# Seven half-size products at the border of layers 0 and 2, PSUM rings by hand, an earlier copy and a reordered start in a four-layer fp32 kernel

## The chip, the cores and the metric

One core of a Trainium2 chip runs the whole program in one launch. The metric is device time in microseconds (us), the median of the runs shown; lower is better. Engines are named as in the profile: PE is TensorE (PEld its weight loads), DVE is VectorE, ACT is ScalarE, POOL is GpSimd and SP is SyncE. L721 is line 721 of the kernel before.

## What is computed

Four images of 512 channels by 1024 tokens pass through four residual layers, all in fp32, each on a group-normalized input:

```python
x = x + attention0(gn(x))   # 8 heads; a head-mixing 8x8 product ahead of the softmax; instance norm; projection and bias
x = x + gate(gn(x))         # channel means -> a 9-qubit circuit simulation -> sigmoid gate per channel
x = x + attention2(gn(x))   # 8 heads; q, k and v with bias; softmax; projection and bias
x = x + memory(gn(x))       # 2048 items; the 8 best per token, softmax over them, weighted sum of rows
```

A projection is a product of a 512x512 weight matrix with a 512x1024 image.

## The kernel before

Channels lie as `[128, 4, 1024]`: partition p and block k hold channel 128k + p. A block is P = 128 channels, NB = 512 is the widest matmul, and KC = 4 blocks.

**Layer 0** goes image by image in STEPS = 32 steps of 32 queries, with seven more steps behind them (LAG = 7). `step` (L1436) writes out by hand what each engine gets in each step: scores, head mixing, exponentials, transposes and products with v, in a software pipeline. Nearly every instruction is wrapped in `pin`, which holds it behind the one traced before it on its engine; so the order on each queue is the order of the code. The products with v of four steps collect in one PSUM bank, `pv_bank`, and `take_out` (L590) copies it to SBUF on ACT in step 34 for tile 6 and in step 38 for tile 7, behind `piece`, which in those steps projects q of the next image. Small results (group sums, key sums, the gate's circuit) share one bank, `pt_bank`, through `small_ps` (L60). Work of the gate for the image before is a generator, `gating` (L861), that is taken one `yield` per step or per projected block (`state["behind"]`).

**The border.** After the last image's steps the kernel projects k (L1148) and v (L1155) of image 0 for layer 2, and then the last image's output of layer 0 (`put_out`, L729), each by 64 half-matmuls of 512 columns (in `put_out` 128 of 256 columns). `instance_norm` (L640) and `norm_quarter` (L666) stand between k and v. `put_out` adds bias and x from DRAM in 128x512 pieces and stores the sum.

**Layer 2.** Here the PSUM tiles come from two pools, `ps_s` (three tiles of two banks) and `ps_m` (two of one bank), opened once layer 0's tiles are released (L1590 to L1595). Score tiles, projections and small results all take the next free tile of `ps_s`. k, v and the output of the images after the first are already made by seven products of half-size blocks (`seven`, L1033): the operands are split in quarters, `weight_sums` (L1007) and `input_sums` (L1000) form sums of quarters on DVE, each of the seven products is 16 half-matmuls, and DVE adds or subtracts each product into the quarters of the result. `seven_out` (L1094) also finishes each quarter as it is complete (`done`, L1122): add x, statistics, store. The order of the products is

```python
SEVEN = (
    (1, ((0, 0, "="), (1, 1, "="))),
    (4, ((0, 0, "+"), (1, 0, "="))),
    (3, ((0, 1, "="), (1, 1, "+"))),
    (5, ((0, 0, "-"), (0, 1, "+"))),
    (2, ((1, 0, "+"), (1, 1, "-"))),
    (7, ((0, 0, "+"),)),
    (6, ((1, 1, "+"),)),
)
```

After `seven_out` the loop goes on with `scores2` (L1165): four score tiles in a row, each read by one exponential on ACT, and then `apply2` (L1206), the products with v of the unit before.

**Start.** `first` (L294) loads image 0 and w_q block by block on SP's queue, while nine small constants are loaded on ACT's queue. For each block DVE takes statistics, two tiny matmuls with `gavg` average them over groups (POOL does the arithmetic between them, L150 to L152, and the power -0.5, L119), DVE normalizes, and the products of q follow block by block (`multiply`, L330).

Of the kernel before, what the change touches and what calls it, by code (L numbers as in the profile page):

```python
# [41 lines left out]
def fast_net(ctx: ExitStack, tc: tile.TileContext, a: dict, out: bass.AP, flag: bass.AP):  # L42
# [19 lines left out]


    def chan(src, name):
        t = const.tile([P, KC], F32, tag=name, name=name)
        nc.scalar.dma_start(out=t, in_=src)
        return t

    gamma = const.tile([P, NH], F32, tag="gamma", name="gamma")
    nc.scalar.dma_start(out=gamma, in_=a["in_gamma"].partition_broadcast(P))  # L70
    beta = const.tile([P, NH], F32, tag="beta", name="beta")
    nc.scalar.dma_start(out=beta, in_=a["in_beta"].partition_broadcast(P))
    bproj = chan(a["b_proj"], "bproj")
    bq2 = chan(a["bq"], "bq2")
    bk2 = chan(a["bk"], "bk2")
    bp2 = chan(a["bp"], "bp2")
    fcb = chan(a["fc_b"], "fcb")

    fcw = const.tile([NQ, C], F32, tag="fcw", name="fcw")
    nc.scalar.dma_start(out=fcw, in_=a["fc_w"])  # L80
    qpar = const.tile([P, NL * NQ], F32, tag="qpar", name="qpar")
    nc.scalar.dma_start(out=qpar, in_=a["q_params"].partition_broadcast(P))
# [3 lines left out]
    ident = const.tile([P, P], F32, tag="ident", name="ident")  # L86
    make_identity(nc, ident)
    ones = const.tile([P, P], F32, tag="ones", name="ones")
    nc.gpsimd.memset(ones, 1.0)
# [13 lines left out]
    )  # L103
    NS = 32
# [71 lines left out]
    def place(at, name):  # L176

        return pairs[at % 3] if at is not None else ps_s.tile([P, 2, NB], F32, tag="sc", name=name)
# [115 lines left out]
    def first():  # L294

        I = img[0]
        xn = I["xn"] = xn_all
        w = I["w_q"] = eight_k([P, KC, C], "w_q0_0", 0)
        for k in range(KC):
            nc.sync.dma_start(out=xn[:, k, :], in_=x_v[0, :, k, :])  # L300
            nc.sync.dma_start(out=w[:, k, :], in_=a["w_q"][:, k, :])
        I["w_k"] = load_w("w_k", "w_k0_0", 1)
        I["w_v"] = load_w("w_v", "w_v0_0", 2)
        q = I["q"] = big("q", "q0_0")
        ybar = I["ybar"] = small.tile([P, KC], F32, tag="ybar", name="ybar0")
        parts, found = {}, {}

        def stats(k):
            mv = small.tile([P, 2], F32, tag="mv0", name=f"mv0_{k}")
            st = small.tile([P, 2, 6], F32, tag="bnst", name=f"st_a0_{k}")  # L310
            for i in range(2):
                pin(nc.vector.bn_stats(st[:, i, :], xn[:, k, i * NB:(i + 1) * NB]))
            pin(nc.vector.bn_aggr(mv, st.rearrange("p i s -> p (i s)")))
            parts[k] = group_coeffs_parts(mv[:, 0:1], mv[:, 1:2], f"a0_{k}")

        def means(k):
            next(parts[k])
            next(parts[k])

        def deviations(k):  # L320
            next(parts[k])
            found[k] = next(parts[k])

        def normalize(k):
            gm, rstd, dm = found[k]
            pin(nc.vector.tensor_scalar(
                xn[:, k, :], xn[:, k, :], gm, rstd, ALU.subtract, ALU.mult))
            pin(nc.gpsimd.tensor_mul(ybar[:, k:k + 1], dm, rstd))

        def multiply(k, m):  # L330
            for n in range(T // NB):
                pin(nc.tensor.matmul(
                    pairs[m][:, n, :],
                    w[:, k, m * P:(m + 1) * P], xn[:, k, n * NB:(n + 1) * NB],
                    start=(k == 0), stop=(k == KC - 1),
                ))

        stats(0)
        means(0)
        stats(1)  # L340
        deviations(0)
        means(1)
        normalize(0)
        for k in range(KC):
            if k + 2 < KC:
                stats(k + 2)
            multiply(k, 0)
            if k + 1 < KC:
                deviations(k + 1)
            multiply(k, 1)  # L350
            if k + 1 < KC:
                normalize(k + 1)
            if k + 2 < KC:
                means(k + 2)
        for m in range(2):
            put_q(q, m)(flat2(pairs[m]))
        for m in (2, 3):
            project(w, tokens(xn), m, m, put_q(q, m))
# [648 lines left out]
    def weight_sums(b, key):  # L1007

        w = img[b][key]
        a11, a21, a12, a22 = quarters(w, H)  # L1010
        s1, s6, s7 = places7[key]
        add7(s1, a11, a22)
        sub7(s7, a12, a22)
        add7(a12, a11, a12)
        sub7(s6, a21, a11)
        add7(a21, a21, a22)
        nc.sync.dma_start(out=w_sums[key], in_=w)
# [15 lines left out]
    def seven(b, key, src, multiply, view, block, begin, done=None):  # L1033
# [3 lines left out]
        b11, t6, t7, b22 = quarters(src, NB)  # L1037
# [3 lines left out]
        for i, (at, uses) in enumerate(SEVEN):  # L1041
            ps = ps_s.tile([P, 2, NB], F32, tag="sc", name=f"{key}_{b}_{at}")
            multiply(ps, *factors[at])
            for *ij, op in uses:
                if op == "=":
                    begin(*ij, ps)
                else:
                    (add7 if op == "+" else sub7)(block(*ij), block(*ij), view(ps))
            if done and i in LAST7:
                done(*LAST7[i][1])  # L1050
            yield

    def by_channels(ps, w, x):
        for m in range(2):
            for k in range(2):
                pin(nc.tensor.matmul(  # L1056
                    ps[:, m, :], w[:, k, m * P:(m + 1) * P], x[:, k, :],
                    start=(k == 0), stop=(k == 1)))

# [105 lines left out]
    def scores2(b, u, before=None):  # L1165
# [14 lines left out]
        for i, t in enumerate(range(t0, t0 + 4)):  # L1180
            sc = ps_s.tile([P, 2, NB], F32, tag="sc", name=f"sc_{nm}_{t}")
# [24 lines left out]
    def apply2(b, u, exp2=None):  # L1206
# [3 lines left out]
        if t0 == 0:  # L1210
            invert2(b)
            I["pv", m, n] = ps_m.tile([P, NB], F32, tag="mm", name=f"pv_c{b}_{m}_{n}")
# [27 lines left out]
    def invert2(b):  # L1240
# [7 lines left out]
        ps = ps_s.tile([P, 2, NB], F32, tag="sc", name=f"rs_{nm}")[:, 0, 0:NS]  # L1248
# [77 lines left out]
    def attention(b, tt, between=None):  # L1326
# [3 lines left out]
        for i, (lo, hi) in enumerate(  # L1330
                ((0, T), (T, T + NB), (T + NB, NI)) if (b, tt) == tiles[-1] else ((0, T), (T, NI))):
            sc = ps_s.tile([P, T], F32, tag="sc", name=f"at_{nm}_{i}")
# [54 lines left out]
    def read_last(b, tt, picked, dg):  # L1387

        got, et, rs, xr = picked
        tp = ps_m.tile([P, KC, P], F32, tag="mm", name=f"stp_{b}_{tt}")  # L1390
# [9 lines left out]
    def read(b, tt, picked):  # L1400
# [9 lines left out]
        tp = ps_m.tile([P, KC, P], F32, tag="mm", name=f"stp_{nm}")  # L1410
# [25 lines left out]
    def step(b, s, mid, piece):  # L1436
# [35 lines left out]
        if tiled:  # L1472
            apply(b, s - LAG)
        if not tiled or s >= STEPS:
            piece(b, s)
# [5 lines left out]
        if tiled and part == 3:  # L1481
            take_out(b, j)
# [57 lines left out]
    for b in range(B):  # L1540
# [18 lines left out]
        for s in range(STEPS, STEPS + LAG):  # L1559
            step(b, s, lambda b, s: next(state["behind"], None),  # L1560
                 lambda b, s: qs[s - STEPS](s + 1) if s < STEPS + KC else None)
            if s == STEPS + KC and not last:
# [5 lines left out]
        for m in range(KC):  # L1568
# [10 lines left out]
        if last:  # L1579
# [5 lines left out]
            for i in range(TC // 2):  # L1585
                take_v2(0, i, i + 2)
            for m in range(KC):
                put_out(b, m, m)

    stage.close()  # L1590
    pairs.clear()
    by_scalar.append(True)
    stage = ctx.enter_context(ExitStack())
    ps_s = stage.enter_context(tc.tile_pool(name="ps_s2", bufs=3, space=PSUM))
    ps_m = stage.enter_context(tc.tile_pool(name="ps_m2", bufs=2, space=PSUM))  # L1595

    def small_ps(name):
        return ps_s.tile([P, 2 * NB], F32, tag="sc", name=name)
# [81 lines left out]
    def check_range():  # L1680
# [3 lines left out]
        tps = ps_m.tile([P, NB], F32, tag="mm", name="tot")  # L1684
# [748 lines left out]
```

## Time and profile before

| | |
|---|---|
| Median of 3 runs | 2556.93 us (2554.43 to 2558.5) |
| The profiled execution | 2558.39 us, span of its records 2556.6 us |
| Granted TensorE clock, mean | 0.998 |
| PE busy | 2503.3 us |
| Seven products in layer 2, third image: k (with one small product in it), v | 24.7 us, 24.3 us |
| One projection of 64 half-matmuls | 27.6 us |

A line of a timeline gives start, duration, engine, line, operation, result and operands, how many instructions are merged, and in brackets the idle time ahead with what ended it. A line of waits gives who waited for whom, the total, how often, and the longest. An fp32 matmul shows as two records, so "x64" is 32 matmuls. A line of the stretches gives for PE, PEld, DVE, ACT and POOL the busy time and the count, then the granted clock, the share of the DMA engines and GB/s. A cold TensorE clock shows as 0.50.

### The profile page before, as it was taken

The numbers are of one execution on the slowest core, as the hardware profiler recorded it, in microseconds if no ns is written. First come the engines' busy times: TensorE is split into PE (matmuls) and PEld (weight loads), VectorE is DVE, ScalarE is ACT, GpSimd is POOL, SyncE is SP. The second block draws the span as 40 slices with busy tenths as digits, with TensorE's granted clock in tenths as the row PEclk, the third lists the DMA queues.
The fourth block names the chain that finished last, engine by engine and source line by source line (L and its number), as shares of the span: only waits on it lengthen the run. The fifth ranks groups of instructions, "written<-read, shape, count | busy, mean of one in ns | idle before, by whom it ended". The sixth has DMA issues, their size and how long they took to land.

```text
span 2556.6 us, 47828 instructions
## 1 busy us (share of the span) xinstructions
PE 2503.3 (98%) x18534; PEld 1180.8 (46%) x18534; DVE 1685.8 (66%) x2785; ACT 985.8 (39%) x1177; POOL 1192.5 (47%) x1700
## 2 busy tenths in 40 slices
PE   8999999999999999999999999999999999999998
PEld 3344534554355534555633533453353344444445
DVE  4599448872688438881267567576657648788875
ACT  1467336651666336651153145125314612121211
POOL 3266415553465425553074147117405617566655
PEclk9999999999999999999999999999999999999999
DMA  2578438872698428982301130121014046767665
GB/s 83 145 207 237 125 120 226 244 211 74 172 243 235 131 82 211 244 248 101 124 16 55 70 112 18 54 83 59 21 54 148 18 130 190 219 186 217 187 184 170
DMA packets 187211, 361.39 MB, mean 141 GB/s; under 512 B 32729, under 2 KB 96217, under 8 KB 182882
## 3 DMA queue, kind: packets, MB, share of 16 engines
q1 hardware_dynamic: 105744, 178.71, 22.6%
q0 software_dynamic: 49152, 142.79, 20.6%
q10 hardware_dynamic: 32082, 36.76, 5.3%
q8 instruction: 149, 2.44, 0.4%
q14 instruction: 84, 0.69, 0.1%
HBM read 186.96 MB, written 36.96 MB: 88 GB/s over the span
## 4 chain that ended last, share of the span: by engine, by line
PE 74%; issue 10%; POOL 7%; DVE 3%; ACT 3%; DMA 2%; POOLq 0%; SPq 0%; ACTq 0%; DVEq 0%
PE pair L192 10%; PE sc_c L1183 9%; PE pv_c L1220 9%; PE pv L532 8%; POOL got L1360 7%; PE pair L467 6%; PE pair L493 5%; PE pt L425 5%; PE pt L721 4%; PE q L192 3%; PE Wk L1056 3%; PE Wv L1063 3%; ACT e L500 2%; PE Wp L1056 2%; PE at L1335 2%
## 5 line engine op out<-in xcount | busy, mean ns | idle before, releaser
L482 POOL DMA_DIRECT2D s<-ss x512 | 258.2, 511 | 399.5 <-PE pair L493 113.4
L506 DVE STREAM_TRANSPOSE eT<-e 128x1024 f32<-128x1024 f32 x256 | 316.5, 1236 | 193.6 <-ACT e L500 193.0
L1360 POOL DMA_INDIRECT got<-in_mem,ix x256 | 279.5, 1092 | 213.2 <-issue 122.1
L1177 ACT ACTIVATE eT<-sc_c 128x1024 f32<-128x1024 f32 x256 | 248.0, 1022 | 330.7 <-PE sc_c L1183 204.8
L521 DVE BATCH_NORM_STATS2 st<-e 128x6 f32<-128x256 f32 x1024 | 350.7, 404 | 0.0
L500 ACT ACTIVATE e<-pair 128x1024 f32<-128x1024 f32 x256 | 250.7, 1022 | 167.5 <-PE pair L493 137.2
L1201 POOL TENSOR_TENSOR e<-eT 128x1024 f32<-128x1024 f32 x96 | 232.3, 2421 | 168.6 <-DVE out L1125 69.5
L467 PE MATMUL pair<-k,q 64*32 64x512 f32 x4096 | 267.4, 598 | 12.7 <-ACT e L500 12.7
L473 ACT COPY ss<-pair 128x1024 f32<-128x1024 f32 x256 | 247.3, 1020 | 77.5 <-DMA s<-ss 37.9
L532 PE MATMUL pv<-eT,v 128*64 128x128 f32 x4096 | 250.7, 276 | 8.9 <-ACT pv L592 8.9
L532 PEld LDWEIGHTS pv<-eT,v 128*64 128x64 f32 x4096 | 221.1, 137 | 76.7 <-issue 54.5
L1183 PE MATMUL sc_c<-q,k 64*128 64x512 f32 x1024 | 240.9, 607 | 3.1 <-DVE xr L684 2.3
L1220 PE MATMUL pv_c<-eT,v 128*64 128x512 f32 x1024 | 233.0, 597 | 0.0
L1202 DVE TENSOR_TENSOR eT<-eT,e 128x1024 f32<-128x1024 f32 x96 | 136.3, 1420 | 146.3 <-POOL e L1201 146.1
L1197 POOL TENSOR_TENSOR eT<-eT 128x1024 f32<-128x1024 f32 x32 | 77.8, 2433 | 206.8 <-ACT eT L1177 202.8
L1407 DVE SCALAR_TENSOR_TENSOR acc<-got,et,acc 128x512 f32<-128x512 f32 x210 | 157.9, 752 | 7.5
L493 PE MATMUL pair<-s,wmix 32*32 32x512 f32 x4096 | 160.6, 600 | 2.3 <-issue 2.1
L1183 PEld LDWEIGHTS sc_c<-q,k 64*128 64x128 f32 x1024 | 93.6, 187 | 141.0 <-issue 71.9
L1340 ACT COPY att<-at 128x1024 f32<-128x1024 f32 (+1 forms) x65 | 64.9, 999 | 219.7 <-PE at L1335 212.9
L467 PEld LDWEIGHTS pair<-k,q 64*32 64x32 f32 x4096 | 57.0, 105 | 179.9 <-ACT e L500 86.2
L1220 PEld LDWEIGHTS pv_c<-eT,v 128*64 128x64 f32 x1024 | 68.0, 137 | 136.8 <-issue 136.8
L1335 PE MATMUL at<-memT,xn_d 128*128 128x512 f32 x256 | 120.7, 594 | 0.0
(335 smaller groups left out, 3431.3 us busy)
## 6 DMA issues: line engine op xcount, KB each, us to landing
s<-ss SPq DMA_DIRECT2D x512, 128.0 KB
s<-ss POOLq DMA_DIRECT2D x512, 128.0 KB
rb<-r POOLq DMA_DIRECT2D x64, 128.0 KB
o<-o SPq DMA_DIRECT2D x32, 256.0 KB
xr<-in_x ACTq DMA_DIRECT2D x32, 256.0 KB
x<-xr SPq DMA_DIRECT2D x32, 256.0 KB
xr_c<-x SPq DMA_DIRECT2D x32, 256.0 KB
rb_c<-r SPq DMA_DIRECT2D x64, 128.0 KB
```

Source lines behind the costliest of these rows:

```text
L192: pin(nc.tensor.matmul(ps[:, n, :], w[:, k, m * P:(m + 1) * P], rhs(k, n), start=(k == 0), stop=(k == KC - 1),))
L467: pin(nc.tensor.matmul(sc[m * NS:(m + 1) * NS, r, :], q[r * HD:(r + 1) * HD, m, s * NS:(s + 1) * NS], k_[r * HD:(r + 1) * HD, m, n * NB:(n ...
L482: pin(relays[side].dma_start(out=s2[2 * m + r::NH], in_=ss[m * NS:(m + 1) * NS, r, :]))
L493: pin(nc.tensor.matmul(mixed(s, r // 2)[t * NS:(t + 1) * NS, r % 2, :].rearrange("p (qq k) -> p qq k", qq=2), wmix[r * NS:(r + 1) * NS], s ...
L500: pin(nc.scalar.activation(e[:, half].rearrange("p r qq k -> p (r qq k)"), flat2(mixed(s, half)), AF.Exp))
L506: pin(nc.vector.transpose(eT[:, j % 2].rearrange("p b (qq i r) x -> p i r qq b x", qq=2, i=4)[:, i, 2 * half:2 * half + 2], e[:, half].rea ...
L521: pin(nc.vector.bn_stats(st[:, i, 2 * half + r, qq, :], e[:, half, r, qq, :]))
L532: pin(nc.tensor.matmul(pv[r * HD:(r + 1) * HD, gp, :], I["v"][:, t, g * HD:(g + 1) * HD], eT[:, j % 2, t, :, 4 * g:4 * g + 4], start=(t == ...
L1177: pin(nc.scalar.activation(e, scs[len(es)], AF.Exp))
L1183: pin(nc.tensor.matmul(sc[:, r, :], I["k"][r * HD:(r + 1) * HD, m, t * P:(t + 1) * P], I["q"][r * HD:(r + 1) * HD, m, n * NB:(n + 1) * NB] ...
L1220: pin(nc.tensor.matmul(pv[r * HD:(r + 1) * HD, :], I["v"][:, t, h * HD:(h + 1) * HD], e[:, r, :], start=(t == 0), stop=(t == TC - 1),))
L1360: pin(nc.gpsimd.indirect_dma_start(out=got[:, i, :], out_offset=None, in_=a["mem"], in_offset=bass.IndirectOffsetOnAxis(ap=ix[:, i:i + 1], ...
```

## The change

1. **Start.** The nine constants are only listed (`held`), and their loads are issued behind those of x and w_q. x's first block is loaded in two halves. `ones` is set first, `ident` later. The arithmetic between the two group matmuls moves from POOL to DVE; the power stays on POOL. Matmuls of `ones` by `ones`, whose result isn't used, run ahead of and between the first steps (`warm`).
2. **take_out** goes ahead of `piece` in the steps from 32 on.
3. **Border.** k and v of image 0 and the last image's output of layer 0 are made by `seven`. Behind step 35 come five weight sums and three input sums; the others go between products. For the output, the sums are made of quarters of the normalized attention (`output_sums`), and `seven_collected` finishes each quarter. The gate's generator is taken seven times in k instead of four.
4. **Rings.** The pools of layer 2 are gone. `next_pair` hands out layer 0's three pairs in turn, `next_bank` its two single banks, and nothing is released in between.

The core of the diff:

```diff
+    turns = [1, 0]
+    def next_pair():
+        turns[0] += 1
+        return pairs[(turns[0] - 1) % 3]
+    later = []
+    def held(shape, name, src):
+        t = const.tile(shape, F32, tag=name, name=name)
+        later.append(lambda: nc.scalar.dma_start(out=t, in_=src))
         return t
...
+        for n in range(2):
+            nc.sync.dma_start(out=xn[:, 0, n * NB:(n + 1) * NB], in_=x_v[0, :, 0, n * NB:(n + 1) * NB])
         for k in range(KC):
-            nc.sync.dma_start(out=xn[:, k, :], in_=x_v[0, :, k, :])
+            if k > 0:
+                nc.sync.dma_start(out=xn[:, k, :], in_=x_v[0, :, k, :])
             nc.sync.dma_start(out=w[:, k, :], in_=a["w_q"][:, k, :])
+        for load in later:
+            load()
...
         def means(k):
-            next(parts[k])
-            next(parts[k])
+            mv = parts[k][0]
+            ps = small_ps(f"gps_a0_{k}")
+            pin(nc.tensor.matmul(ps[:, 0:1], gavg, mv[:, 0:1], start=True, stop=True))
+            dm, sq, gm = (column(name, k) for name in ("dm", "gsq", "gm"))
+            pin(nc.vector.tensor_sub(dm, mv[:, 0:1], ps[:, 0:1]))
+            pin(nc.vector.scalar_tensor_tensor(sq, dm, dm, mv[:, 1:2], ALU.mult, ALU.add))
+            pin(nc.vector.tensor_copy(gm, ps[:, 0:1]))
...
+        def warm(times):
+            for _ in range(times):
+                pin(nc.tensor.matmul(pairs[2][:, 0, 0:P], ones, ones, start=True, stop=True))
...
-        stats(0)
+        warm(11)
+        for i in range(2):
+            stats(0, i)
         means(0)
-        stats(1)
+        stats(1, 0)
+        warm(2)
         deviations(0)
+        stats(1, 1)
+        warm(2)
+        normalize(0)
         means(1)
-        normalize(0)
+        warm(2)
...
         for i, (at, uses) in enumerate(SEVEN):
-            ps = ps_s.tile([P, 2, NB], F32, tag="sc", name=f"{key}_{b}_{at}")
+            ps = next_pair()
...
+    def seven_collected(b):
...
+        def done(i, j):
+            for m in range(2 * i, 2 * i + 2):
+                part = dst[:, m, j * NB:(j + 1) * NB]
+                add7(part, part, rows.pop((m, j)))
+                pin(nc.vector.bn_stats(I["stb"][:, m, j, :], part))
+                if (i, j) in ((0, 0), (1, 1)):
+                    pin(nc.vector.bn_aggr(
+                        mv[:, m, :], I["stb"][:, m].rearrange("p i s -> p (i s)")))
+            nc.sync.dma_start(
+                out=x1[b][:, 2 * i:2 * i + 2, j * NB:(j + 1) * NB], in_=block(i, j))
...
         for i, t in enumerate(range(t0, t0 + 4)):
-            sc = ps_s.tile([P, 2, NB], F32, tag="sc", name=f"sc_{nm}_{t}")
+            sc = next_pair()
...
+        if s >= STEPS and tiled and part == 3:
+            take_out(b, j)
         if not tiled or s >= STEPS:
             piece(b, s)
...
-        if tiled and part == 3:
+        if tiled and part == 3 and s < STEPS:
             take_out(b, j)
...
+            if last and s == STEPS + 3:
+                border_places()
+                first7, rest7 = input_sums(nxt["xn"])
+                weight_sums(0, "Wk", False)
+                for fn in first7:
+                    fn()
...
+            for i, _ in enumerate(seven_k(0)):
+                if i == 0:
+                    for fn in rest7:
+                        fn()
+                if i == 2:
+                    weight_sums(0, "Wv", False)
+                if i == 4:
+                    weight_sums(b, "w_p", False)
+                next(state["behind"], None)
...
-            for i in range(TC // 2):
-                take_v2(0, i, i + 2)
-            for m in range(KC):
-                put_out(b, m, m)
-
-    stage.close()
-    pairs.clear()
+            sums7 = output_sums(b)
+            for i, _ in enumerate(seven_v(0)):
+                if i >= 2:
+                    for fn in next(sums7):
+                        fn()
+            seven_collected(b)
...
-    ps_s = stage.enter_context(tc.tile_pool(name="ps_s2", bufs=3, space=PSUM))
-    ps_m = stage.enter_context(tc.tile_pool(name="ps_m2", bufs=2, space=PSUM))
+    def next_bank():
+        turns[1] += 1
+        return (pv_bank, pt_bank)[turns[1] % 2]
```

## The prediction

> **What bounds it now.** I read the page's busy times, TensorE's waits, and then the timeline of the three places that the change touches. TensorE is busy throughout, so only its own work and its own waits count.
> ```profile
> PE 2503.3 (98%) x18534; PEld 1180.8 (46%) x18534; DVE 1685.8 (66%) x2785; ACT 985.8 (39%) x1177; POOL 1192.5 (47%) x1700
> ...
> PE 74%; issue 10%; POOL 7%; DVE 3%; ACT 3%; DMA 2%; POOLq 0%; SPq 0%; ACTq 0%; DVEq 0%
> ```
> The waits (us in total, times, longest) of TensorE; under them SP's longest:
> ```profile
> PE pv L532 <- ACT pv L592: 8.9, 15, 1.6
> PE sc_c L1183 <- DVE xr L684: 2.3, 1, 2.3
> PE Wk L1056 <- ACT k L1073: 2.0, 1, 2.0
> ...
> SPq L301 <- DMA bproj<-in_b_proj: 6.1, 1, 6.1
> ```
> Timeline of the start and of the border (start, us, engine, line, operation): TensorE, then VectorE.
> ```profile
> 11.31 3.78 PE L332 MATMUL pair<-xn_all,w_q 128*128 128x512 f32 x4 [0.97 <-DVE xn_all L326]
> 15.10 1.96 PE L332 MATMUL pair<-xn_all,w_q 128*128 128x512 f32 x4
> ...
> 1174.21 0.39 PE L886 MATMUL pt<-amp,turn 128*128 128x4 f32 x2
> 1174.53 3.71 PE L532 MATMUL pv<-eT,v 128*64 128x128 f32 x64
> 1178.86 0.38 PE L891 MATMUL pt<-amp,turn 128*128 128x2 f32 x2 [0.62 <-POOL amp L883]
> 1179.33 13.98 PE L192 MATMUL pair<-xn_all,Wk_n 128*128 128x512 f32 x32
> ...
> 1237.38 27.79 PE L745 MATMUL pair<-eT 128*128 128x256 f32 x128
> 1267.48 8.83 PE L1183 MATMUL sc_c<-q,k 64*128 64x512 f32 x32 [2.32 <-DVE xr L684]
> ...
> 1172.28 1.28 DVE L1145 TENSOR_SCALAR q<-pair,bq 128x1024 f32<-128x1024 f32 x1 [7.73 <-PE pair L192]
> 1173.48 0.35 DVE L559 RECIPROCAL ri<-pt 128x32 f32<-128x32 f32 x1
> 1174.63 0.16 DVE L130 COPY amp<-pt 128x4 f32<-128x4 f32 x1 [0.35 <-PE pt L886]
> ```
> The same four matmuls take 3.78 cold and 1.96 warm. At the border VectorE answers TensorE within a microsecond. k, v and the last output are 27.6 to 27.9 us of matmul each, then 2.32 of waiting. In stretches of 2 us, just after that wait (the figure after POOL's is the granted clock):
> ```profile
> 1267.00:1269.00 2.00, 1.52 (x4) 0.75 (x6) 1.48 (x5) 0.00 (x0) 0.00 (x0) 0.68 0.59 226
> 1269.00:1271.00 2.00, 2.00 (x8) 0.99 (x6) 0.00 (x0) 1.02 (x1) 0.00 (x0) 0.50 0.64 151
> ```
> End of a layer-2 output by seven products:
> ```profile
> 1491.85 3.60 PE L1056 MATMUL Wp<-eT 128*128 128x512 f32 x8
> 1495.38 4.69 PE L1183 MATMUL sc_c<-q,k 64*128 64x512 f32 x16
> 1500.00 3.65 PE L1220 MATMUL pv_c<-eT,v 128*64 128x512 f32 x16
> ...
> 1495.37 1.20 DVE L993 TENSOR_TENSOR out<-out,Wp 128x1024 f32<-128x1024 f32 x1
> 1499.84 1.17 DVE L993 TENSOR_TENSOR out<-out,Wp 128x1024 f32<-128x1024 f32 x1
> ```
> All four score tiles are done by 1500.0, though the last product's bank is read only from 1499.84 to 1501.01: the pool gave the third tile another bank.
>
> [...]
>
> **The change, part by part** (against the profiled 2558.39 us, span 2556.6; it lies 1.5 above the median, 2556.93).
>
> (1) Start. SP's second weight load waits 6.1 us for a small constant; the constants now go last, and x's first block comes in halves. VectorE begins on x at 5.60; I take 0.6 earlier for each of its two statistics and so an end of the first block's statistics near 5.8 instead of 7.13 (bounds 5.3 and 7.1). From there it is: group mean matmul 0.55, three small VectorE operations 0.6, second matmul 0.4 beside the next block's half (0.65), epsilon 0.15, power on POOL 0.6, second half and its aggregate 0.85 beside that, normalize 0.8: first product at about 9.6, not 11.31, gain 1.7. The power stays on POOL; what POOL loses (three operations of 0.19 and their handovers) is replaced by VectorE's. The warm-up matmuls (11, then 2 three times) fill TensorE's idle time: gain 3.78 - 1.96 = 1.8, or 0 if the clock falls back in between. Afterwards VectorE needs 3.65 per block and TensorE about 3.9, so the lead lasts. whp lands by 39, circuit's VectorE work ends at 56.4, k's first copy at 57.6, and its bank is wanted at 59.1: still hidden. **-3.6** (-1 to -5).
>
> (2) take_out ahead of the projection at step 34: the copy on ScalarE no longer stands behind q's copy. Waits removed for images 0 to 2: 1.59 + 1.47 + 1.47. Image 3's q goes through VectorE. **-4.5**.
>
> (3) Border. Each of three projections falls from 64 to 56 half-matmuls: 27.6 x 7/8 = 24.2, so -10.3 in all. Added ahead of them, on VectorE, after L1145: five weight sums 128x512 (0.69, in a row 3.35) and three input sums 128x1024 (1.22, in a row 3.5): 6.85 us. Behind them in the queue stand L559, L561 and L130. L886 writes the bank that L559 reads: it can't start before 1173.56 + 6.85 + 0.35 = 1180.8, where it started at 1174.21, and two of the pv groups (3.71) and L891 stand behind it. L130 comes at 1181.4; POOL then needs its issue (0.6), L605 (1.8) and the amplitude's operations (2.1), as it did between 1174.12 and 1178.8: L891 near 1186, or 1186.6 with the pv groups at half clock after 6.5 us idle. k begins at 1187.0 instead of 1179.3: +7.7. Bounds: 0, if other work ran there, and 9.
>
> k: 24.2, L901 0.5, L916 1.0 between products. VectorE: eight block sums from PSUM (1.22), two input sums, ten weight sums: about 19 us, beside it; but the last sum, L645 and POOL stand before L651: 2.2 after k's end. v begins at 1187.0 + 25.7 + 2.2 = 1214.9. In v, VectorE has 12 x 1.22 and twenty sums of 128x256 with runs of 16 (no row; between half and all of 128x512's 0.684; taken 0.38): 22.2, ends 3.2 late, harmless. The output begins at 1239.1, ends at 1263.3. Its VectorE work (8 x 1.22, eight times 0.69 + 0.69, aggregates) falls behind TensorE. From the output's begin: the fourth product ends at +13.8, its two sums at +16.15, the finished block (add and statistics of two halves, 2.7) at +18.85; fifth: sums +21.2, block +23.9; the sixth product (+20.7) has its sum at +25.1 and its block, aggregates and all 3.1, at +28.2; so the last product (+24.2) has its sum at +29.4. With a ring the third score tile takes the last product's pair: it waits from +26.05 to +29.45. pv then begins at +34.9, +36.3 with a chance of 0.8 for 3.4 us at half clock (1.7). That is 1275.4 where it was 1276.25: **-0.9** for all of (3), the pool's wait and its clock loss included; against before, k begins 7.7 later, v 5.1, the output 1.7. x's loads go through SP as the stores do; slots come free 3 us before use.
>
> (4) Rings in layer 2. The same third tile: three times it waits until 1501.05 and not 1497.7. Two tiles of 0.95 later pv starts at 1502.95, not 1500.0: +2.9, and 3.35 us idle is longer than the 2.32 that cost the clock: +1.7 x 0.8. 3 x 4.3 = **+12.8** (0 to 14). Elsewhere the ring asks for a tile whose reader is done (the exps end 0.5 us before pv does): 0.
>
> (5) Three more steps of the gate are taken in k, so its group sum leaves the first product gap of image 1, and product 4 finds a free pair: **-2.0** (0 to -2). The weights aren't stored three times: SP only, 0.
>
> Sum: -3.6 - 4.5 - 0.9 + 12.8 - 2.0 = +1.8: 2560.2 by the profiled run, **2558.7** from the median.
>
> **Rivals.** (B) No ring waits, because VectorE gets to the last sum in time: -12.8, and -4.7 in (3): 2541.2. The 4.5 us between L993's two lines speak against it. (C) The sums at the border run before L1145, where VectorE idles 7.73 us: 2558.7 - 7.7 = 2551.0. Against it: each is pinned behind the one before it. (D) Slower: a clock lost in the middle of a wait costs two windows, not one[...]; four waits by 1.7 make +6.8: 2565.5. [...] against, the 3.4 us it lasted at 1267.8. (E) B and C together, or the output sums hidden wholly: 2533.5.
>
> **How the numbers follow.** Chances: mine 0.56 (own range 2553 to 2564), B 0.12, C 0.14, D 0.12, E 0.06. The range reaches from B to D, 2541 to 2566. About 0.2% (5.1 us) is what a measurement can tell from no change. Faster: B, E, half of C, 0.02 of mine: 0.27. Slower: 0.10 of D, 0.12 of mine: 0.22. Same: 0.51.
>
> **What would show it.** First L332 line near 9.6 with 1.96; no wait over 0.3 at L592 in three images; a gap of 6 us before L886 and the eight sums ahead of L559; 24.2 per seven products; a wait of 3.4 us on L993's last sum in the third score tile at all four places, with clock 0.5 after it. If L886 isn't late, or the third tile isn't, the forecast is wrong by 8 or 13 us.

## The result, and the profile after

After: median 2568.61 us of 6 runs (2564.96 to 2570.74). Before: 2556.26 in six runs, the three above among them (2554.43 to 2559.41). The ratio is 1.0047, 95% interval 1.0035 to 1.0059: slower by 12.4 us. The forecast was 2558.7, and the result lies 2.6 above its range.

The profiled execution of after: span 2567.2. Its busy times and the shares of its chain:

```profile
PE 2508.8 (98%) x18568; PEld 1190.1 (46%) x18568; DVE 1725.9 (67%) x2857; ACT 992.2 (39%) x1189; POOL 1188.9 (46%) x1688
...
PE 72%; issue 8%; POOL 7%; DMA 5%; DVE 5%; ACT 2%; SPq 0%; POOLq 0%; ACTq 0%; DVEq 0%
```

TensorE has more busy time (2508.8 against 2503.3) though 24 of the border's 192 half-matmuls are gone: the warm-up matmuls and work at half clock stand in for them. The longest new and old waits of TensorE, then SP's:

```profile
PE pair L1301 <- DVE out L1028: 9.9, 3, 3.3
PE pt L921 <- DVE ri L594: 6.4, 1, 6.4
PE pv L567 <- ACT pv L627: 4.3, 12, 1.0
PE pair L1301 <- DVE sum L1028: 3.2, 1, 3.2
PE pt L936 <- POOL pr L931: 2.7, 1, 2.7
```
```profile
SPq L306 <- DMA gamma<-in_in_gamma: 2.2, 1, 2.2
...
SPq L307 <- DMA bproj<-in_b_proj: 1.4, 1, 1.4
```

The wait for `take_out`'s copy (L567) fell from 8.9 to 4.3. New are the waits of the score tiles (L1301) for VectorE, 13.1 in all, that of the gate's first rotation (L921), and one of the gate's sums (L936). SP still waits for constants.

A ledger, read from the start of the same TensorE instruction in both timelines, shows where the time came from:

| up to | before | after | difference | this stretch |
|---|---|---|---|---|
| q's last blocks of image 0 | 28.26 | 27.80 | -0.5 | start -0.5 |
| the key sum behind the last q of layer 2 | 1172.08 | 1167.22 | -4.9 | take_out -4.4 |
| first product with v of layer 2 | 1276.25 | 1275.93 | -0.3 | border +4.5 |
| first of the seven products for k, image 1 | 1413.58 | 1413.60 | 0.0 | +0.3 |
| first score unit of image 1 | 1467.51 | 1465.92 | -1.6 | gate's step -1.6 |
| third score unit of image 1 | 1503.58 | 1507.56 | +4.0 | ring +5.6 |
| the same, image 2 | 1722.69 | 1732.53 | +9.8 | ring +5.9 |
| the same, image 3 | 1941.82 | 1956.01 | +14.2 | ring +4.4 |
| last transpose of layer 3 | 2528.82 | 2543.01 | +14.2 | 0 |
| end of the span | 2556.6 | 2567.2 | +10.6 | the last tile -3.6 |

The last row isn't put down to the change: from that transpose to the end the profiled execution of before took 27.8 us, those of the changed kernel and of all the experiments 23.3 to 25.0, one with before's own layer 3 (e4) among them. Whether most executions of before end like the profiled one isn't known; +14.2 and +10.6 both lie within the interval of the medians' +12.4 (8.9 to 15.1).

A ledger compares one execution with one other. The nine kernels profiled here that have this start reach the first mark at 27.15 to 28.45 (before, and e4 with before's start: 28.26 and 28.48), and the twelve with the early copy take 1139 to 1143 for the second stretch (after 1139.4, before 1143.8). So these two rows are known only within some 1 and 4 us.

**Start.** TensorE, then VectorE:

```profile
9.53 0.38 PE L332 MATMUL pt<-mv,gavg 128*128 128x1 f32 x2 [1.51 <-DVE mv L324]
...
10.77 3.09 PE L360 MATMUL pair<-xn_all,w_q 128*128 128x512 f32 x4
```
```profile
7.88 0.69 DVE L322 BATCH_NORM_STATS2 st_a<-xn_all 128x6 f32<-128x512 f32 x1 [0.85 <-DMA xn_all<-in_x]
8.49 0.14 DVE L344 TENSOR_SCALAR gve_a<-pt 128x1 f32<-128x1 f32 x1
```

The first product begins at 10.77, not 9.6, and is cold for most of its length (3.09, with the clock at 0.50 up to 13.20; warm is 1.96). The epsilon of the first block (L344) stands behind statistics of the second block, which wait for its arrival at 7.88.

**Border.** TensorE, VectorE and GpSimd:

```profile
1175.77 0.56 PE L921 MATMUL pt<-amp,turn 128*128 128x4 f32 x2 [6.35 <-DVE ri L594]
1176.26 5.79 PE L567 MATMUL pv<-eT,v 128*64 128x128 f32 x64
...
1182.45 3.68 PE L1092 MATMUL pair<-eT 128*128 128x512 f32 x8
...
1192.31 0.35 PE L936 MATMUL pt<-pr,signs 128*9 128x1 f32 x8 [2.75 <-POOL pr L931]
...
1192.79 5.40 PE L1092 MATMUL pair<-eT,Wk_n 128*128 128x512 f32 x8
```
```profile
1167.42 1.28 DVE L1263 TENSOR_SCALAR q<-pair,bq 128x1024 f32<-128x1024 f32 x1 [7.73 <-PE pair L195]
...
1175.28 0.35 DVE L594 RECIPROCAL ri<-pt 128x32 f32<-128x32 f32 x1
```
```profile
1188.39 3.59 POOL L640 TENSOR_TENSOR o<-pv,rb 64x256 f32<-64x256 f32 x4
1192.06 0.20 POOL L931 TENSOR_TENSOR pr<-amp 128x4 f32<-128x4 f32 x1
```

The eight sums lie between q's copy and the reciprocal, as forecast; the idle 7.73 us ahead of that copy stayed empty. Not forecast: the gate's squares (L931) come behind four multiplications of the attention's output (L640); in before the order was the other way round. L931 isn't pinned, and no line of the diff moves it. TensorE waits 2.75 for it, and the product behind takes 5.40, not 3.70.

**Layer 2.** The first of its output borders on TensorE and VectorE, and stretches of 2 us (the figure after POOL's is the granted clock):

```profile
1493.78 2.38 PE L1301 MATMUL pair<-q,k 64*128 64x512 f32 x8
1499.46 3.78 PE L1301 MATMUL pair<-q,k 64*128 64x512 f32 x8 [3.30 <-DVE out L1028]
1503.17 4.45 PE L1338 MATMUL pt<-eT,v 128*64 128x512 f32 x16
```
```profile
1498.24 1.17 DVE L1028 TENSOR_TENSOR out<-out,pair 128x1024 f32<-128x1024 f32 x1
```
```profile
1496.00:1498.00 2.00, 0.16 (x2) 0.00 (x0) 1.93 (x4) 1.06 (x2) 0.64 (x1) 1.00 0.99 365
1498.00:1500.00 2.00, 0.54 (x2) 0.50 (x4) 1.63 (x4) 0.00 (x0) 1.71 (x1) 0.50 0.88 294
1500.00:1502.00 2.00, 2.00 (x6) 0.68 (x4) 1.97 (x3) 0.00 (x0) 0.00 (x0) 0.50 0.38 119
1502.00:1504.00 2.00, 2.00 (x6) 0.29 (x4) 1.90 (x5) 0.00 (x0) 0.00 (x0) 0.50 0.00 0
1504.00:1506.00 2.00, 2.00 (x10) 0.66 (x8) 0.18 (x1) 0.85 (x1) 0.00 (x0) 0.79 0.68 262
```

The third score tile waits for VectorE's last sum, as forecast. But the clock is at 0.50 from 1498 to beyond 1504. In the traces of before and after such a stretch lasts 3.41 us, called a window here, or twice that, 6.83 (unless the trace ends in it): this one, from 1498.00 to 1504.83, is two windows and not one.

### The profile page after: what moved, and what is told of

The parts are those of the page before. It is cut to its first block, busy times and chain, and to the rows that moved or that the text cites. A ratio compares the mean times of both kernels' runs of the same rounds, so it can differ in the third digit from the quotient of the medians.

```text
span 2567.2 us, 47940 instructions
## 1 busy us (share of the span) xinstructions
PE 2508.8 (98%) x18568; PEld 1190.1 (46%) x18568; DVE 1725.9 (67%) x2857; ACT 992.2 (39%) x1189; POOL 1188.9 (46%) x1688
## 3 DMA queue, kind: packets, MB, share of 16 engines
q8 instruction: 149, 2.44, 0.4%
## 4 chain that ended last, share of the span: by engine, by line
PE 72%; issue 8%; POOL 7%; DMA 5%; DVE 5%; ACT 2%; SPq 0%; POOLq 0%; ACTq 0%; DVEq 0%
PE pair L195 14%; PE pair L1301 9%; PE pv L567 8%; POOL got L1478 6%; PE pair L502 6%; PE pair L1092 5%; PE pair L528 5%; PE pt L460 5%; PE pt L1338 4%; PE pv L1338 4%; PE pair L1181 4%; PE pt L756 4%; DMA got<-in_mem,ix 3%; ACT e L535 2%; PE pair L1453 2%
## 5 line engine op out<-in xcount | busy, mean ns | idle before, releaser
L1295 ACT ACTIVATE eT<-pair 128x1024 f32<-128x1024 f32 x256 | 248.7, 1022 | 324.6 <-PE pair L1301 192.4
L1301 PE MATMUL pair<-q,k 64*128 64x512 f32 x1024 | 245.6, 618 | 13.4 <-DVE out L1028 9.9
L567 PE MATMUL pv<-eT,v 128*64 128x128 f32 x4096 | 252.7, 277 | 4.3 <-ACT pv L627 4.3
L567 PEld LDWEIGHTS pv<-eT,v 128*64 128x64 f32 x4096 | 223.2, 138 | 71.9 <-issue 55.2
L1320 DVE TENSOR_TENSOR eT<-eT,e 128x1024 f32<-128x1024 f32 x96 | 130.1, 1355 | 167.2 <-POOL e L1319 167.1
L1301 PEld LDWEIGHTS pair<-q,k 64*128 64x128 f32 x1024 | 94.8, 190 | 153.0 <-issue 71.7
L1458 ACT COPY att<-pair 128x1024 f32<-128x1024 f32 (+1 forms) x65 | 64.9, 999 | 220.9 <-PE pair L1453 220.8
L1453 PE MATMUL pair<-memT,xn_d 128*128 128x512 f32 x256 | 120.7, 594 | 0.0
L1453 PE MATMUL pair<-memT,eT 128*128 128x512 f32 x256 | 120.4, 593 | 0.0
L1453 PE MATMUL pair<-eT 128*128 128x512 f32 x256 | 120.3, 592 | 0.0
```

Source lines behind the costliest of these rows:

```text
L567: pin(nc.tensor.matmul(pv[r * HD:(r + 1) * HD, gp, :], I["v"][:, t, g * HD:(g + 1) * HD], eT[:, j % 2, t, :, 4 * g:4 * g + 4], start=(t == ...
L1295: pin(nc.scalar.activation(e, scs[len(es)], AF.Exp))
L1301: pin(nc.tensor.matmul(sc[:, r, :], I["k"][r * HD:(r + 1) * HD, m, t * P:(t + 1) * P], I["q"][r * HD:(r + 1) * HD, m, n * NB:(n + 1) * NB] ...
L1453: pin(nc.tensor.matmul(sc[:, i0 - lo:i0 - lo + NB], xn3[b][:, k, tt * P:(tt + 1) * P], memT[k][:, i0:i0 + NB], start=(k == 0), stop=(k == ...
```

## The experiments

All times are medians, against 2568.6 for after and 2556 to 2557 for the runs of before beside them; the interval is that of the ratio to before. Numbers of lines differ by up to twelve from one kernel to the next.

**e1, another pair for the score tiles.**

```diff
+    def spare_last():
+        t = turns[0]
+        spare[:] = [pairs[t % 3], pairs[(t + 1) % 3]] * 2
+        turns[0] += 2
     def next_pair():
+        if spare:
+            return spare.pop(0)
...
         run_out(seven(b, "Wp", I["o"], by_channels, lambda ps: ps, block, begin, done))
+        spare_last()
```
(and the same behind `seven_collected`'s products)

> The changed kernel, but the four score tiles behind the last of seven products take the two other pairs in turn, never the pair of that last product. Theory (the ring makes the third tile wait for VectorE's last sum, and the wait costs clock behind it): the waits of 3.18 and three times 3.30 us are gone, the clock stays at 1.00 there; counted from the traces 5.6 + 5.9 + 4.4 us come back at the three borders in layer 2 and about 4.9 (3.2 and half a window of 3.4) at the border of layers 0 and 2: 20.8 less than 2568.6, so 2548. Rival (VectorE's backlog is what counts and the wait only moves to the next user of that pair or to the exponentials): the products with v begin no earlier, at most the clock comes back, 2562 to 2568.

Measured 2550.78, ratio 0.9977 (0.9968 to 0.9987): 17.8 less. The first output border of layer 2:

```profile
1491.50 4.69 PE L1311 MATMUL pair<-q,k 64*128 64x512 f32 x16
1496.12 3.65 PE L1348 MATMUL pt<-eT,v 128*64 128x512 f32 x16
```

The wait is gone, and the matmuls take what they took in before (4.69 and 3.65); from the first score tile to the first product with v are 4.62 us, as in before (4.62), where after took 9.39. At the border of layers 0 and 2 the gain is 3.4 and not 4.9: 0.93 of waiting for the same sum remains, now at the fifth use. The ring, by itself, cost more than the whole loss of 12.4.

**e5, the wait kept and filled.**

```diff
             sc = next_pair()
+            if i == 2:
+                for _ in range(fill[0]):
+                    pin(nc.tensor.matmul(
+                        (pv_bank, pt_bank)[(turns[1] + 1) % 2][:, 0:P], ones, ones, start=True, stop=True))
+                fill[0] = 0
```
(`fill[0] = 10` behind `seven_out`'s products)

> The changed kernel, with ten unused matmuls of ones by ones (128x128, about 2.4 us) written into the idle bank between the second and third score tile at the three borders in layer 2; the wait for VectorE's last sum stays. Theory (beside the wait of 3.30 us the clock is lost for one or two windows, because TensorE idles): the third tile begins no earlier, TensorE's waits there fall to about 0.9, the clock stays at 1.00, and of the 5.6 + 5.9 + 4.4 us only three times 3.3 are left: 6 less, 2562.6. Rival (the low clock comes from something else than idling, or the wait alone made the loss): the clock falls all the same, 2568 to 2570.

Measured 2562.54, ratio 1.0025 (1.0017 to 1.0033): 6.1 less.

```profile
1494.21 2.38 PE L1309 MATMUL pair<-q,k 64*128 64x512 f32 x8
1496.52 2.50 PE L1305 MATMUL pt<-ones 128*128 128x128 f32 x20
1499.89 1.99 PE L1309 MATMUL pair<-q,k 64*128 64x512 f32 x8 [0.87 <-DVE out L1028]
1501.81 3.65 PE L1346 MATMUL pt<-eT,v 128*64 128x512 f32 x16
```

The third tile begins 5.68 after the first, just as in after (1499.46 - 1493.78), and then takes 1.99 and not 3.78. From the first score tile to the next score unit a border takes 11.2 in e5, 8.2 in before, and 13.8, 14.1 and 12.6 in after. So of the ring's 15.8 us in layer 2 8.9 are the delay that the waits make while the clock stays whole, and 6.9 are lost clock (6.1 between the medians), and the clock is lost because TensorE idles: with 2.50 us of the gap filled it stayed at 1.00.

**e9 and c5, the last sum ahead of the block work.**

```diff
-            if done and i in LAST7:
+            if done and i in LAST7 and i != 5:
+                if i == 6:
+                    done(*LAST7[5][1])
                 done(*LAST7[i][1])
```
(e9: after with this alone; c5: with the edits of e1 and e2 too)

> The changed kernel with its ring as it is, but VectorE adds the last product before it finishes the block of the product ahead of it (x, statistics), at all four borders. Theory (the wait needs both: a ring that gives the third score tile the last product's pair, and 2.9 us of block work ahead of that product's sum in VectorE's queue): the last sum ends about 2.9 us earlier, the third tile waits 0.4 instead of 3.3, the clock stays, and the same 15.9 at the three borders in layer 2 and about 3.4 at the border of layers 0 and 2 come back as with the other pairs: 2549. Rival (block work that comes later holds up the next image's statistics or the row buffers instead, and the waits appear further on): 2555 to 2568.

> The changed kernel with all three repairs: other pairs for the score tiles, the border's first sums one step earlier, the last product's sum ahead of the block work. Theory (the first and the third repair take away the same waits, so together they give hardly more than one; left are 0.9 + 0.2 us at the border of layers 0 and 2): 2537.8 - 1.1 = 2536.7, not to be told from c2_both's 2537.8. Rival (the repairs add up): 2520.

Measured 2560.97, ratio 1.0013 (1.0006 to 1.0020), 7.6 less than after, for e9 and 2547.70, 0.9963 (0.9949 to 0.9978), for c5; both expectations fell. The wait of the third tile is gone, but two units later there is a new one, at all four borders. c5's TensorE and VectorE:

```profile
1502.50 0.31 PE L1381 MATMUL pair<-s_c,same 128*64 128x32 f32 x4 [1.99 <-DVE s_c L1367]
```
```profile
1485.27 2.60 DVE L1254 SCALAR_TENSOR_TENSOR out<-xr_c,s,out 128x512 f32<-128x512 f32 x1
...
1489.37 3.37 DVE L1332 TENSOR_TENSOR eT<-eT,e 128x1024 f32<-128x1024 f32 x1
...
1493.51 2.23 DVE L1254 SCALAR_TENSOR_TENSOR out<-xr_c,s,out 128x512 f32<-128x512 f32 x1
```

The block work now begins while GpSimd adds exponentials (from 1484.96, 1489.20 and 1492.83, for 2.35 to 2.46 each). There it took 2.60 and 2.23, against 0.70 to 0.75 outside, and VectorE's own sum of exponentials (L1332) 3.37, against 1.22. Why they are stretched isn't shown. The key sums end 21.0 us after the first score tile behind the border, in c2 (below), where the first block's work comes earlier and only two operations are stretched (1.96 and 3.27), 17.4; TensorE wants them at 19.1. The waits of 2.0 to 2.4, four times, 8.4 in all, make most of the 10 us between c2 and c5. The rival was right: the wait moved.

**e2, the first sums one step earlier.**

```diff
-            if last and s == STEPS + 3:
+            if last and s == STEPS + 2:
```

> The changed kernel, but the border's eight first sums are written one step earlier, ahead of the last block's copy of q on VectorE. Theory (the eight sums hold back the reciprocal, and with it the matmul that writes the bank it reads): they fill VectorE's idle 7.7 us, TensorE's wait of 6.4 us falls under 0.5 and the half clock after it goes too; k begins 8 us earlier. The gate's squared amplitudes on GpSimd come only 6.6 us earlier, so the wait of 2.7 us ahead of the third product grows by about 1.3: 7 less, 2561.5. Rival (the sums then wait for something else, as the place they write is still read by the products with v): q's last copy comes late, k begins no earlier, 2567 to 2570.

Measured 2557.30, ratio 0.9999 (0.9990 to 1.0008): 11.3 less, 4 more than expected. VectorE, TensorE and GpSimd at the border:

```profile
1164.33 4.14 DVE L1028 TENSOR_TENSOR eT<-xn_all 128x1024 f32<-128x1024 f32 x3
1168.39 1.27 DVE L1263 TENSOR_SCALAR q<-pair,bq 128x1024 f32<-128x1024 f32 x1
1169.59 0.34 DVE L594 RECIPROCAL ri<-pt 128x32 f32<-128x32 f32 x1
```
```profile
1170.28 0.39 PE L921 MATMUL pt<-amp,turn 128*128 128x4 f32 x2
...
1175.42 3.68 PE L1092 MATMUL pair<-eT 128*128 128x512 f32 x8
```
```profile
1181.63 0.20 POOL L931 TENSOR_TENSOR pr<-amp 128x4 f32<-128x4 f32 x1
1181.78 3.60 POOL L640 TENSOR_TENSOR o<-pv,rb 64x256 f32<-64x256 f32 x4
```

The sums end just as q's block does, nothing waits for the reciprocal, and k begins 7.3 behind the key sum's matmul (1168.14), not 15.2. The expectation that L936's wait would grow was wrong: the squares stand ahead of the four multiplications again, and the wait is gone. From the key sum to the first product with v are now 96.3 us: after took 108.7, before 104.2.

**e6, the gate one product later.**

```diff
-                next(state["behind"], None)
+                if i > 0:
+                    next(state["behind"], None)
```

> The changed kernel, but the gate's generator is taken behind the second and later products of k only, six times instead of seven. Theory (what the border cost beyond the forecast is the wait of 2.75 us for the gate's squares on GpSimd ahead of the third product, and half a window of clock behind it, 1.7): the small product comes behind the third product of k, finds the squares done, and 4.4 come back: 2564.2. Rival (the matmuls behind it are slow for another reason, or the wait comes again at the next step of the gate): 2567 or more.

Measured 2568.23, ratio 1.0047 (1.0031 to 1.0063): no gain that the medians show. In the trace L936's wait is gone and v begins 43.6 behind the key sum, not 47.9: the 4.4 are there. Most of them were given back: the wait of 1.8 ahead of v, which cost no clock in after, cost a window at half clock here (5.39 for the first product behind it, where e2 has 3.70: 1.7), and with one gate step fewer at the border the wait of 1.96 in image 1 is back, where after had 0.69 (1.4 up to the first score unit). The 1.2 that are left are less than the medians can tell.

```profile
1211.00 0.39 PE L686 MATMUL pt<-ssqh,ones 128*128 128x8 f32 x2 [1.83 <-POOL ssqh L683]
1211.24 5.39 PE L1181 MATMUL pair<-eT 128*128 128x256 f32 x16
...
1417.44 7.13 PE L1092 MATMUL pair<-sums,Wk 128*128 128x512 f32 x16 [1.96 <-ACT k L1191]
```

**e7, the old border**: no first sums, no seven products for k, v and the last output.

```diff
-            if last and s == STEPS + 3:
+            if False:
...
-        for m in () if last else range(KC):
+        for m in range(KC):
...
-            seven_collected(b)
+            for i in range(TC // 2):
+                take_v2(0, i, i + 2)
+            for m in range(KC):
+                put_out(b, m, m)
```

> The changed kernel with the border of before: k, v and the last output by 64 half-matmuls each, no sums, the gate taken four times in k; start, copy and rings as changed. Theory (the new border, as it was built, costs 4.5 us more than the old one, counted between the last block of q and the first product with v): these 4.5 come back, the ring gives the first score tile another pair than the one that the old output's last addition reads, which saves its wait of 2.3 us and half a window of clock, 4 in all, and the gate's small product in image 1 costs 1.6 again: 2568.6 - 4.5 - 4 + 1.6 = 2561.7. Rival (the seven products save what was forecast, 0.9, and the loss is elsewhere): 2567 or more.

Measured 2564.64, ratio 1.0028 (1.0017 to 1.0038): 4.0 less than after, between the two. From the key sum to the first product with v it takes 102.4 against 108.7: 6.3 came back, not 8.5, since v ran for a window at half clock (0.50 in the stretch from 1207 to 1209), as it hadn't in before (29.4 against 27.7). The wait of 1.96 in image 1 is back. In image 2 the third tile waited 6.19, as a row of x came late for the block work; the profiled execution lies 3.6 above the median, so this wait may not be in most others. That the new border cost more than the old one, as it was built, holds; its size in the total is settled only within some 3 us.

**e4, take_out alone**, in the kernel before.

```diff
+        if s >= STEPS and tiled and part == 3:
+            take_out(b, j)
         if not tiled or s >= STEPS:
             piece(b, s)
...
-        if tiled and part == 3:
+        if tiled and part == 3 and s < STEPS:
             take_out(b, j)
```

> The kernel before with one part of the change: take_out ahead of the projection in the steps from 32 on. Theory: the three waits of 1.5 to 1.6 us for the copy go, 4.4 in all, and nothing comes for them: 2551.9 where before is 2556.3. Rival (part of the saving in the trace of the changed kernel came from its other start): 2554 to 2556.

Measured 2550.80, ratio 0.9981 (0.9974 to 0.9988): 5.3 less, and 4.4 lies within the interval (3.1 to 6.6). The trace has the same wait for the copy as after, 4.3 instead of 8.9, but it doesn't show the gain where it was looked for. From q's last blocks of image 0 to the last key sum e4 takes 1142.8 us, before 1143.8, after 1139.4: the products of the head mixing (L493) wait 2.1 longer for what they read, 1.6 of it in one wait; where the rest went isn't shown. Of the 5.3 us between the two profiled executions 4.5 lie in the last tile of layer 3. So less waiting and a lower median are shown; that the one makes the whole of the other isn't.

**e3, the constants on SP's queue**, behind x and w_q.

```diff
-        later.append(lambda: nc.scalar.dma_start(out=t, in_=src))
+        later.append(lambda: nc.sync.dma_start(out=t, in_=src))
```

> The changed kernel, but the nine constants are loaded from SP's queue, behind x and w_q, instead of from ScalarE's queue, which had nothing ahead of them. Theory (they were still issued at once and SP's issues of x's later blocks waited 2.2 us for gamma and 1.4 us for bproj): those waits are gone, the third block of x lands 2 to 3 us earlier than 13.4, the fourth products of q end 1 to 3 us earlier, 2566.5. Rival (the bytes ahead of it set when the third block lands): it lands within 0.5 us of 13.4 and the time stays at 2568.6.

Measured 2569.13, ratio 1.0054 (1.0041 to 1.0067): no gain. SP's waits ahead of x's blocks are gone and all nine loads are issued by 5.9. But VectorE and TensorE:

```profile
10.25 0.69 DVE L322 BATCH_NORM_STATS2 st_a<-xn_all 128x6 f32<-128x512 f32 x1 [3.40 <-DMA xn_all<-in_x]
```
```profile
13.34 3.62 PE L360 MATMUL pair<-xn_all,w_q 128*128 128x512 f32 x4
```

The second block is there at 10.25, not 7.88, and the first product comes 2.6 later for it. By 8.0 us both kernels had moved the same amount (1.46 MB here, 1.43 in after), more than x's first two blocks and w_q's first (1.31 MB); here part of it belonged to later loads. From these amounts I estimate that the waits for the constants had kept the early loads alone on the way; no other run tries it.

**c2 and c3, the repairs together.** c2 is after with the edits of e1 and e2. c3 also orders the start so that a block's statistics stand behind the normalizing of the block before:

```diff
         deviations(0)
-        stats(1, 1)
-        warm(2)
+        warm(5)
         normalize(0)
-        means(1)
+        for i in range(2):
+            stats(1, i)
...
             if k + 1 < KC:
                 normalize(k + 1)
+            if k + 2 < KC:
+                for i in range(2):
+                    stats(k + 2, i)
```
(`means(k + 1)` and `deviations(k + 1)` stand ahead of and behind a half of block k's products)

> The changed kernel with both repairs: score tiles on the two other pairs, and the border's first sums one step earlier. Theory (the two losses lie in different places and add up): 2568.6 - 17.8 - 11.3 = 2539.5, 16.7 under the kernel before. Rival (they share a cause, VectorE's backlog at the border): less than their sum, 2543 to 2548.

> As c2_both, and at the start the statistics of x's next block stand behind the normalizing of the block before on VectorE, with the means and deviations between the halves of a block's products. Theory (the first product waits for the second block of x, whose statistics stand ahead of the first block's epsilon in VectorE's queue): the first product begins at 9.2 and not at 10.8; 0.7 us of idle time is added ahead of each later block, so the last product of q's first half ends only about 0.8 earlier than 27.9. Rival (the arrival of x's third block at about 13 sets it all): it ends at 27.9 or later. In the total this can't be told from c2_both.

Measured 2537.81, ratio 0.9927 (0.9914 to 0.9940), for c2 and 2539.07, 0.9931 (0.9918 to 0.9943), for c3. The two repairs add up (29.1 expected, 30.8 measured), and c2 is 19.1 under the kernel before. In c3 the first product begins at 9.29; in c2 at 10.98, and in the nine traces with after's start at 10.29 to 10.98. So it was the queue's order that held the first product. q's next blocks begin at 27.27 against 28.25 in c2, but the nine lie between 27.15 and 28.45: that anything is left of the gain by then isn't shown.

## Why the prediction was wrong

Its sum was +1.8 for -3.6 - 4.5 - 0.9 + 12.8 - 2.0. The ledger has -0.5 - 4.4 + 4.5 + 15.8 - 1.6 and 0.3 of small things: +14.2. Against the medians the miss is 9.9.

**(1) Start: wrong, by 3.1 in the ledger** (2.3 to 3.8 with the spread named below it). Two steps failed. "The constants now go last" took the order of the program for the order in time: they are on ScalarE's queue, which has nothing ahead of them, and they were issued at once, the first at 0.81 us as in before. And "second half and its aggregate 0.85 beside that" took the second block to be there; it wasn't, and since its statistics stand ahead of the first block's epsilon, its arrival set the first product (10.77; e3 moved the arrival by 2.4 and the product by 2.6, c3 took it out of the way and got 9.29). The warm-up matmuls gained little: with 1.51 of waiting between them the clock fell back (0.50 from 9.79), a bound that the prediction had named. No run leaves them out.

**(2) take_out: right in the wait, its total not settled.** 4.5 forecast, and 4.6 less waiting for the copy in all twelve traces that have it early. The stretch gains 4.4 in after, but 0.9 to 4.9 in the twelve, 3.0 in the mean, as the head mixing waits 0.3 to 2.1 longer in them; the medians of e4 have 5.3 (3.1 to 6.6).

**(3) Border: right in its mechanism, wrong in its sum, by 5.4.** The sums ahead of the reciprocal, the wait of L921 (6.35, forecast 6.5), the half clock behind it (0.50 from 1173.73 to 1180.56), k's begin (+8.0, forecast +7.7), v's wait for GpSimd (1.8, forecast 2.2) and the third tile's wait at the end (3.18, forecast 3.4) all came. The step that failed is "L901 0.5 ... between products": the gate's sums got there a product earlier than their squares. That wait of 2.75 and the window behind it, 1.7, are 4.4 of the 5.4; e6 took them out and v began 4.3 earlier. The squares come late because they stand behind the four multiplications on GpSimd. That is so in all six traces in which the sums stand ahead of the reciprocal, and in none of the other seven; what orders an instruction that isn't pinned no run shows. e2, with the sums in the idle stretch, shows what the border is worth when it is not held up: 7.9 less than before, the ring's wait included, and 11.3 less in c2.

**(4) Rings: right in its mechanism and place, mis-sized by 3.0.** The waits are 3.30 (3.35 forecast), three times, and the delay that they make with the clock whole is 3.0 each (2.9 forecast). The term that was too small is the clock: 0.8 times 1.7 for each was 4.1 in all, and the traces of after and e5 give 6.9. Rival (D) had this, as an estimate that no trace of before shows: after two of the three waits the clock was low for two windows (6.83 us), after the third for one. It put the time at 2565.5; of its 6.8 more, 2.8 came in layer 2, and the rest of the miss is (1) and (3). How many windows a wait of 3.30 costs differs (two, two and one in after, none at the first of e3's borders; last section), so that this term could only be given as a range.

**(5) The gate: right,** 1.6 of 2.0. With three steps more the wait is 0.69, with two more (e6) or none (e7) 1.96.

**Rivals.** (B) fell: at none of the four places did VectorE get to the last sum in time. (C) fell, as each sum is pinned where it was written, and e2 shows that it was a matter of one step. The range had been drawn to (D) alone; a start without gain and one unforeseen wait at the border, each of 3 to 5 us, were not in it.

## What to carry to other kernels

When a pool of buffers becomes a fixed ring, write down who reads each slot last and when: a pool gives the next user the slot that is free, a ring the one whose turn it is, and here that cost 16 us where all the saved matmuls brought 8 to 11. Put new work into a queue's idle stretch by looking at what stands behind it, and where a wait is repaired, read the next two units as well: reordering the same queue only moved it. Loads written later in the program on another, empty queue weren't later: the first constant was issued at 0.81 us, as in before.

## What the runs showed that was not expected

**The clock fell after waits much shorter than a window, and one wait cost none, one or two windows.** Waits of 0.89 (with tiny matmuls just before it), 1.83 and 1.96 us cost a window at half clock in one kernel and nothing in another, though the instructions around them are the same:

```profile
1208.80 0.39 PE L651 MATMUL pt<-ssqh,ones 128*128 128x8 f32 x2 [0.89 <-POOL ssqh L648]
1209.05 29.41 PE L204 MATMUL pair<-Wv_n,xn_all 128*128 128x512 f32 x64
```

This is e4, the kernel before but for `take_out`; in before the same lines have 0.89 and 27.71. Behind the wait of 1.83 ahead of v the first product took 5.39 in e6 and 3.70 in e2; behind that of 1.96 in image 1 the clock was 0.50 from 1415 to 1417 in e7, and 1.00 throughout in before. In before and in after the stretches at 0.50 begin a whole number of windows apart (374 between 1267.72 and 2544.30 in before; 95 between 1173.73 and 1498.00 in after), so a grid of 3.41 us can be laid over each. The same border and the same wait of 3.30 in the windows of such a grid, after first, then e3:

```profile
1494.59:1498.00 3.41, 1.45 (x6) 0.30 (x4) 3.27 (x6) 2.05 (x2) 0.64 (x1) 1.00 1.02 382
1498.00:1501.41 3.41, 1.95 (x6) 0.92 (x8) 3.04 (x5) 0.00 (x0) 1.71 (x1) 0.50 0.74 242
1501.41:1504.83 3.42, 3.42 (x10) 0.79 (x8) 2.64 (x6) 0.00 (x0) 0.00 (x0) 0.50 0.20 78
```
```profile
1498.68:1502.09 3.41, 1.71 (x8) 0.30 (x4) 3.27 (x6) 2.05 (x2) 0.38 (x1) 1.00 1.04 393
1502.09:1505.50 3.41, 1.69 (x8) 0.69 (x8) 3.05 (x5) 0.00 (x0) 1.97 (x1) 1.00 0.80 261
```

The first figure behind the comma is TensorE's busy time. In after the grid cuts the wait into 1.96 and 1.46 us of idle time and two windows are lost; in e3 it cuts it into 1.70 and 1.72, and none is. At after's second border, with 2.44 and 0.86, two are lost, at its third, with 2.75 and 0.55, one. The grid doesn't lie alike in both: a window begins at 1498.00 in after and at 1498.68 in e3.

In before and after, from 24 us on, each of the eight windows at full clock with 2.17 us or more of idle time was followed by one at 0.50. Of the five with 1.51 to 1.96 those with 1.51 and 1.96 were, and those with 1.59, 1.60 and 1.89 weren't; none with less was, though in e4 the wait of 0.89 was followed by 0.50. Behind windows at 0.50 with 0.86, 1.46 and 2.04 of idle time came another, behind those with 0.55 or less none. What sets the outcome between 0.89 and 1.96 isn't settled. A few unused matmuls in the gap (e5) kept the clock at 1.00 with 0.87 us of idle time left.

**With the later loads issued sooner, x's second block came later** (e3): VectorE began on x's second block at 10.25, against 7.88 in after, though its load was issued 2.2 us earlier.
